# The three 3x3 convolutions of an attention block as matmuls over 42 channels x 3 tap rows

## The chip, the cores and the metric

One NeuronCore of a Trainium2 chip. Its engines are TensorE (PE; its weight loads are listed as PEld), VectorE (DVE), ScalarE (ACT), GpSimd (POOL) and SyncE (SP), which here only issues DMAs. Everything is float32. The metric is the device time of one execution in microseconds, the median over runs; lower is better.

## The reference, cut to what matters

The input is `x`, 8 images of 384 channels of 32 x 32 pixels. Four residual layers follow one another, each on a group norm of its input: attention with depthwise convolutions (layer 0), a mixture of experts, a ternary convolution block, and a deformable attention. Only the front of layer 0 is touched here:

```python
def _bn(x, g, b):                       # batch norm: statistics over images and pixels
    m = x.mean(axis=(0, 2, 3), keepdims=True); v = x.var(axis=(0, 2, 3), keepdims=True)
    return (x - m) * lax.rsqrt(v + EPS) * g[None, :, None, None] + b[None, :, None, None]

def _dwproj(x, dw, g, b, pw):           # depthwise 3x3, batch norm, gelu, 1x1 projection
    y = lax.conv_general_dilated(x, dw, (1, 1), ((1, 1), (1, 1)), feature_group_count=C, ...)
    y = jax.nn.gelu(_bn(y, g, b), approximate=False)
    return jnp.einsum('oc,bchw->bohw', pw, y)

q, k, v = (_dwproj(x, dw, g, b, pw) for each of three sets of weights)
# then softmax attention of 8 heads over the 1024 pixels, and an output projection
```

Each channel is convolved three times (for q, k and v) with nine weights of its own. No channel mixes with another. The batch norm needs the statistics of all eight images before the first gelu, so the convolutions are a stage of their own: every image is convolved, the raw result goes to DRAM, and only then does attention begin.

## The kernel before, in words

The kernel is written in a tile language that places instructions on the engines' queues; each engine takes its own queue in order, and waits are put in where a tile is read or its buffer is used again. `load_image` (line 145) brings an image in as three chunks of 128 channels x 1024 pixels, one DMA each. All DMAs are issued by SP.

The first stage works image by image:

- `gn_stats` (lines 77 to 121) makes the group norm's scale and shift: `bn_stats` and `bn_aggr` on DVE (lines 83 and 84), seven tiny matmuls `gna` (line 89), three small DVE steps (lines 97 to 101), seven tiny matmuls `gnb` (line 105), a power on POOL (line 75) and one more DVE step.
- `affine` (line 125, ACT) writes the normalized image into a zero-bordered tile `pad` of 34 x 34 pixels a channel. There are two `pad` tiles, used in turn.
- For each chunk of 128 channels, the k convolution runs on TensorE: nine products with diagonal 128 x 128 matrices `diag`, accumulated in a PSUM bank of 512 pixels, two banks a chunk (line 209), copied out by ACT (line 216). The matrices are built once on POOL (line 184).
- The q and v convolutions of the same chunk run on DVE, nine instructions each over 128 x 1024 pixels: line 223 for the first tap, line 225 for the other eight.
- `bn_stats` on DVE takes the statistics of each result (line 229), and a DMA stores it to `raw` in DRAM (line 232).

After the last image, `bn_params` (line 133 on) turns the statistics into scale and shift, which lie with the channels on partitions as the gelu wants them. Attention then loads its weights (lines 252 and 255), loads `g` from `raw` (line 145), applies gelu on ACT (line 265) and starts with the value projection `pv` on TensorE (line 275). From there on each of the eight images takes some 447 us in attention, and the other three layers follow.

Of the kernel before, what the change touches and what calls it, by code (L numbers as in the profile page):

```python
# [7 lines left out]
F32 = mybir.dt.float32  # L8
# [5 lines left out]
N = H * W            # tokens of one image  # L14
P = 128
KC = C // P          # channel chunks
HALF = N // 2        # one PSUM bank of fp32
NT8 = N // P         # token chunks of one image

# layer 0: attention of 8 heads of 48, each padded to 64 rows  # L20
NH0, HD0, NPAIR0 = 8, 48, 4
# layer 1: 4 experts
NE = 4
# layer 3: 6 heads of 64 over 16 x 16 sampled keys, 3 offset groups
NPAIR3, HS, LS, NG = 3, 16, 256, 3

# group norm: 32 groups of 12 channels; the chunk pairs that share a group
GN_C = C // 32
GN_PAIRS = {0: (0, 1), 1: (0, 1, 2), 2: (1, 2)}
RNE = 12582912.0     # 1.5 * 2^23: adding and subtracting rounds to the nearest even integer  # L30
# [3 lines left out]
def tile_kernel(ctx: ExitStack, tc: tile.TileContext, i: dict, out: bass.AP):  # L34
# [17 lines left out]
    def evac(dst, src):  # L52
        """A copy out of PSUM, by the Scalar and the Vector engine in turn."""
        flip[0] ^= 1
        if flip[0]:
            nc.scalar.copy(dst, src)  # L56
        else:
            nc.vector.tensor_copy(dst, src)  # L58
# [14 lines left out]
    def rsqrt(dst, var, n):  # L73
        """dst = var ** -0.5 for [P, n] tiles."""
        nc.gpsimd.tensor_tensor(dst, var, mhalf[:, :n], ALU.pow)

    def gn_stats(x, tag, pool=None):
        """Scale and shift [P, 2, KC] of the group norm of one image [P, KC, N]."""
# [6 lines left out]
        # group mean of the channels' means and variances  # L85
# [12 lines left out]
        # spread of the channels' means around the group's  # L98
# [30 lines left out]
    def bn_params(st, n, g, b, name):  # L129
        """Scale and shift [P, n] of a batch norm from the statistics [P, n, 2B, 6]."""  # L130
        mv = const.tile([P, n, 2], F32, name=f"bnmv_{name}")
        for j in range(n):
            nc.vector.bn_aggr(mv[:, j, :], st[:, j, :, :].rearrange("p a b -> p (a b)"))
        sc = const.tile([P, n], F32, name=f"bnsc_{name}")
        sh = const.tile([P, n], F32, name=f"bnsh_{name}")
        nc.vector.tensor_scalar(sh, mv[:, :, 1], 1e-5, None, ALU.add)
        rsqrt(sc, sh, n)
        nc.vector.tensor_tensor(sc, sc, g, ALU.mult)
        nc.vector.tensor_tensor(sh, mv[:, :, 0], sc, ALU.mult)
        nc.vector.tensor_tensor(sh, b, sh, ALU.subtract)  # L140
        return sc, sh
# [8 lines left out]
    def ternary(dst, w, shape, scale_ap):  # L150
        """dst = w + (clip(round(w * scale), -1, 1) - w)."""
# [10 lines left out]
    # ------------------------------------------------------------------  # L162
    # layer 0, part 1: group norm, three depthwise convolutions, their statistics
    # ------------------------------------------------------------------
    dw0 = load_const("dw0")        # [P, 3 convs, KC, 9]
    gb0 = load_const("gb0")        # [P, 2, 9]
    cst = const.tile([P, 9, 2 * B, 6], F32, name="cst")
    raw = [
        [dram.tile([P, KC, N], F32, name=f"raw{v}_{b}") for b in range(B)] for v in range(3)
    ]  # L170
    with ExitStack() as pa:
        wa = pa.enter_context(tc.tile_pool(name="a_w", bufs=1))
        xa = pa.enter_context(tc.tile_pool(name="a_x", bufs=2))
        ya = pa.enter_context(tc.tile_pool(name="a_y", bufs=3))
# [5 lines left out]
        # the key convolution runs on the tensor engine, as nine diagonal products  # L180
        diag = wa.tile([P, KC, 9, P], F32, name="diag")
        for c in range(KC):
            for t in range(9):
                nc.gpsimd.tensor_scalar(
                    diag[:, c, t, :], ident, dw0[:, 1, c, t : t + 1], 1.0, ALU.mult, ALU.mult
                )
        for b in range(B):
# [3 lines left out]
            pad = pads[b % 2]  # L191
            for c in range(KC):
# [6 lines left out]
            for c in range(KC):  # L199
                for v in (1, 0, 2):  # L200
                    y = ya.tile([P, H, W], F32, tag=f"y{v}", name=f"y{v}_{b}_{c}")
                    yf = y.rearrange("p h w -> p (h w)")
                    if v == 1:
                        for h in range(2):
                            pk = bank(f"pk{b}_{c}_{h}")
                            for t in range(9):
                                dy, dx = divmod(t, 3)
                                r0 = h * (H // 2) + dy
                                nc.tensor.matmul(  # L209
                                    pk,  # L210
                                    lhsT=diag[:, c, t, :],
                                    rhs=pad[:, c, r0 : r0 + H // 2, dx : dx + W],
                                    start=(t == 0),
                                    stop=(t == 8),
                                )
                            nc.scalar.copy(yf[:, h * HALF : (h + 1) * HALF], pk)
                    else:
                        for t in range(9):
                            dy, dx = divmod(t, 3)
                            src = pad[:, c, dy : dy + H, dx : dx + W]  # L220
                            w1 = dw0[:, v, c, t : t + 1]
                            if t == 0:
                                nc.vector.tensor_scalar(y, src, w1, None, ALU.mult)
                            else:
                                nc.vector.scalar_tensor_tensor(  # L225
                                    y, src, w1, y, ALU.mult, ALU.add
                                )
                    for h in range(2):
                        nc.vector.bn_stats(
                            cst[:, v * KC + c, 2 * b + h, :], yf[:, h * HALF : (h + 1) * HALF]  # L230
                        )
                    nc.sync.dma_start(out=raw[v][b][:, c, :], in_=yf)
    sc0, sh0 = bn_params(cst, 9, gb0[:, 0, :], gb0[:, 1, :], "qkv")

    # ------------------------------------------------------------------
    # layer 0, part 2: gelu, projections, attention, output projection
    # ------------------------------------------------------------------
    ost = const.tile([P, KC, 2 * B, 6], F32, name="ost")
    o_dram = [dram.tile([P, KC, N], F32, name=f"o_{b}") for b in range(B)]
    with ExitStack() as pb:  # L240
# [17 lines left out]
        for b in range(B):  # L258
            act = []
            for v in range(3):  # L260
                g = gp.tile([P, KC, N], F32, tag=f"g{v}", name=f"g{v}_{b}", bufs=2 if v < 2 else 1)
                load_image(g, raw[v][b])
# [7 lines left out]
            # values, tokens on partitions  # L270
# [91 lines left out]
    gbo = load_const("gbo")        # [P, 2, KC]  # L362
    sco, sho = bn_params(ost, KC, gbo[:, 0, :], gbo[:, 1, :], "out")

    # ------------------------------------------------------------------
    # weights of layers 1 to 3
    # ------------------------------------------------------------------
# [11 lines left out]
    # layer 2: ternary weights  # L379
# [4 lines left out]
    with tc.tile_pool(name="w2_raw", bufs=1) as wr:  # L384
        dw2 = load_w("dw2", wr)    # [P, KC, 9]
        pw2 = load_w("pw2", wr)    # [P, KC, C]
# [17 lines left out]
    # layer 3  # L404
# [5 lines left out]
    # bn3 columns: dw_b, bn_w, bn_b, bn_mean, bn_var  # L410
# [6 lines left out]
    # ------------------------------------------------------------------  # L417
    # layer 0's end and layer 1's routing
    # ------------------------------------------------------------------
    x1_dram = [dram.tile([P, KC, N], F32, name=f"x1_{b}") for b in range(B)]  # L420
    wk = wd.tile([P, B, 2, NT8], F32, name="wk")        # the two choices' weights by token
    pres = wd.tile([P, 2, NE], F32, name="pres")        # whether an expert is ever a choice
# [6 lines left out]
    with ExitStack() as pc:  # L429
# [3 lines left out]
        for b in range(B):  # L433
# [46 lines left out]
            for k in range(2):  # L480
# [4 lines left out]
                # of equal scores the lower index comes first  # L485
# [24 lines left out]
    # ------------------------------------------------------------------  # L510
    # layers 1 to 3, image by image
    # ------------------------------------------------------------------
# [6 lines left out]
    def layer1(b):  # L519
# [5 lines left out]
        # coefficients of the experts by token, then turned so that tokens lie along the free axis  # L525
# [84 lines left out]
    def layer3(b, xt):  # L610
# [15 lines left out]
        # the image with positions on partitions, to sample from  # L626
# [8 lines left out]
        # offsets: 5x5 depthwise convolution of stride 2  # L635
# [24 lines left out]
        # offsets and modulation of every sample, on all partitions  # L660
# [17 lines left out]
        # bilinear weights of a position for a sample: max(0, 1-|dy|) * max(0, 1-|dx|)  # L678
# [18 lines left out]
        # keys, scaled, and values with samples on partitions  # L697
# [85 lines left out]
def _chunks(w):  # L783
    """[K, M] -> [P, K / P, M]: rows by chunk of partitions."""
# [6 lines left out]
def _cols(v):  # L791
    """[C] -> [P, C / P]."""
# [3 lines left out]
def _layouts(a):  # L796
# [9 lines left out]
    # layer 0  # L806
    L["dw0"] = np.stack(
        [a[f"L0_conv_dw_{n}"].reshape(KC, P, 9).transpose(1, 0, 2) for n in "qkv"], axis=1
    )
    L["gb0"] = np.stack(  # L810
        [np.concatenate([_cols(a[f"L0_conv_{t}_{n}"]) for n in "qkv"], axis=1) for t in "gb"],
        axis=1,
    )
# [8 lines left out]
    # layer 1  # L822
# [8 lines left out]
    # layer 2  # L831
    L["dw2"] = a["L2_conv_w_dw"].reshape(KC, P, 9).transpose(1, 0, 2)
    L["pw2"] = _chunks(a["L2_conv_w_pw"].reshape(C, C).T)
    # layer 3
# [38 lines left out]
```

## Time and profile before

| | |
|---|---|
| median of 5 runs | 7619.18 us (7588.29 to 7625.57) |
| profiled execution, its own time | 7618.04 us |
| span of its trace, first to last instruction | 7616.3 us |
| mean granted TensorE clock | 0.862 |
| first convolution matmul starts | 22.41 us |
| last convolution matmul record begins | before 640.6 us |
| first matmul of attention (`pv`) | 685.82 us |

A trace is one execution. A group in it is named by line, engine and operation; "x864" counts the records of the group. A float32 matmul and its weight load each leave two records, so the 432 convolution matmuls of line 209 show as 864. "Idle before" is the time for which the engine did nothing ahead of the group, and what ended it. In the view of windows each engine's busy time in a stretch stands beside its instruction count, then the granted TensorE clock, the busy share of the 16 DMA engines and the GB/s that they moved. The records of matmuls overlap, so a matmul's own duration is longer than the step from one to the next.

### The profile page before, as it was taken

The numbers are of one execution on the slowest core, as the hardware profiler recorded it, in microseconds if no ns is written. First come the engines' busy times: TensorE is split into PE (matmuls) and PEld (weight loads), VectorE is DVE, ScalarE is ACT, GpSimd is POOL, SyncE is SP. The second block draws the span as 40 slices with busy tenths as digits, with TensorE's granted clock in tenths as the row PEclk, the third lists the DMA queues.
The fourth block names the chain that finished last, engine by engine and source line by source line (L and its number), as shares of the span: only waits on it lengthen the run. The fifth ranks groups of instructions, "written<-read, shape, count | busy, mean of one in ns | idle before, by whom it ended". The sixth has DMA issues, their size and how long they took to land.

```text
span 7616.3 us, 48331 instructions
## 1 busy us (share of the span) xinstructions
PE 6415.6 (84%) x18164; PEld 3010.5 (40%) x18164; DVE 3017.6 (40%) x4739; ACT 1957.4 (26%) x3391; POOL 913.6 (12%) x740
## 2 busy tenths in 40 slices
PE   6766999999999999999999569696969686878777
PEld 3333444444444444444444454343434343434333
DVE  8996333333333333333333321424242424242443
ACT  0002233323323332332222221222212121213123
POOL 0000111111111111111111000010101010101011
PEclk8887988898988889898898669898989898988888
DMA  2112000000000000000000420000000000000000
GB/s 92 77 69 97 0 25 9 17 17 0 33 0 25 9 17 17 1 34 0 6 3 4 164 100 0 9 9 9 9 9 9 9 9 9 9 9 9 0 9 9
DMA packets 52521, 178.74 MB, mean 23 GB/s; under 512 B 7352, under 2 KB 7612, under 8 KB 52032
## 3 DMA queue, kind: packets, MB, share of 16 engines
q1 hardware_dynamic: 52288, 175.65, 6.1%
q8 instruction: 144, 2.36, 0.1%
q14 instruction: 89, 0.73, 0.0%
HBM read 100.13 MB, written 75.50 MB: 23 GB/s over the span
## 4 chain that ended last, share of the span: by engine, by line
PE 73%; DVE 17%; ACT 5%; POOL 3%; issue 2%; DMA 1%; SPq 0%; ACTq 0%; DVEq 0%; POOLq 0%
PE pav L338 13%; PE s L316 12%; PE tp L332 8%; PE ph L556 7%; PE y L569 7%; PE pq L291 5%; DVE y L225 4%; DVE off L653 3%; DVE y L593 3%; PE po L351 2%; PE pv L275 2%; PE pav L754 2%; PE pk L209 2%; DVE mx L321 2%; PE pf L764 2%
## 5 line engine op out<-in xcount | busy, mean ns | idle before, releaser
L316 PE MATMUL s<-qk,qk 64*128 64x512 f32 x2048 | 1100.6, 681 | 97.8 <-ACT p L324 97.8
L338 PE MATMUL pav<-pt,vt 128*64 128x512 f32 x2048 | 962.4, 625 | 0.0
L327 POOL TENSOR_SCALAR p<-p,ri 128x1024 f32<-128x1024 f32 x512 | 571.3, 1119 | 2973.3 <-DVE ri L326 2968.7
L58 DVE COPY pt<-tp 128x512 f32<-128x512 f32 x608 | 419.2, 690 | 1052.1 <-PE tp L332 882.5
L321 DVE TENSOR_REDUCE mx<-s 128x1 f32<-128x1024 f32 x512 | 626.9, 1224 | 374.6 <-PE s L316 373.2
L332 PE MATMUL tp<-ident_sb,p 128*128 128x128 f32 x4096 | 676.2, 326 | 86.2 <-POOL p L327 86.2
L332 PEld LDWEIGHTS tp<-ident_sb,p 128*128 128x128 f32 x4096 | 564.9, 168 | 433.5 <-POOL p L327 274.4
L324 ACT ACTIVATE p<-s,mx 128x1024 f32<-128x1024 f32 x512 | 570.9, 1115 | 563.7 <-DVE mx L321 389.7
L56 ACT COPY pt<-tp 128x512 f32<-128x512 f32 x608 | 352.5, 585 | 893.5 <-PE tp L332 724.7
L316 PEld LDWEIGHTS s<-qk,qk 64*128 64x128 f32 x2048 | 353.3, 200 | 561.1 <-issue 302.8
L338 PEld LDWEIGHTS pav<-pt,vt 128*64 128x64 f32 x2048 | 284.0, 145 | 704.7 <-issue 659.0
L556 PE MATMUL ph<-h,w_sb 128*128 128x512 f32 x1152 | 558.8, 616 | 0.0
L569 PE MATMUL y<-hd,w_sb 128*128 128x512 f32 x1152 | 547.0, 612 | 0.0
L567 DVE TENSOR_TENSOR hd<-hd,cb 128x512 f32<-128x512 f32 x192 | 132.6, 691 | 850.6 <-ACT hd L564 850.6
L225 DVE SCALAR_TENSOR_TENSOR y<-pad,dw_sb,y 128x1024 f32<-128x1024 f32 x384 | 466.4, 1274 | 0.0
L209 PE MATMUL pk<-pad,diag 128*128 128x512 f32 x864 | 393.2, 619 | 23.0 <-ACT pad L125 23.0
L564 ACT ACTIVATE hd<-ph,b_sb 128x512 f32<-128x512 f32 x192 | 132.0, 687 | 925.8 <-PE ph L556 925.8
L556 PEld LDWEIGHTS ph<-h,w_sb 128*128 128x128 f32 x1152 | 221.0, 196 | 310.2 <-issue 267.5
L569 PEld LDWEIGHTS y<-hd,w_sb 128*128 128x128 f32 x1152 | 211.5, 193 | 299.9 <-issue 203.7
L602 PE MATMUL pw<-y,upw 128*128 128x512 f32 x288 | 164.7, 738 | 173.3 <-DVE y L593 173.3
L209 PEld LDWEIGHTS pk<-pad,diag 128*128 128x128 f32 x864 | 170.2, 198 | 240.1 <-issue 214.8
L741 POOL TENSOR_TENSOR p<-p,ri 128x1024 f32<-128x1024 f32 x96 | 181.0, 1893 | 497.8 <-DVE ri L740 494.1
(209 smaller groups left out, 6110.1 us busy)
## 6 DMA issues: line engine op xcount, KB each, us to landing
raw<-y SPq DMA_DIRECT2D x72, 512.0 KB, 2.6
g<-raw SPq DMA_DIRECT2D x72, 512.0 KB, 4.9
xa<-in_x_dram SPq DMA_DIRECT2D x24, 512.0 KB, 4.5
o<-ot SPq DMA_DIRECT2D x48, 256.0 KB, 2.0
xc<-in_x_dram SPq DMA_DIRECT2D x24, 512.0 KB, 4.4
oc<-o SPq DMA_DIRECT2D x24, 512.0 KB, 6.3
x<-xc SPq DMA_DIRECT2D x24, 512.0 KB, 2.9
x<-x SPq DMA_DIRECT2D x24, 512.0 KB, 4.7
```

What stands on the lines that cost most here:

```text
L58: nc.vector.tensor_copy(dst, src)
L209: nc.tensor.matmul(pk, lhsT=diag[:, c, t, :], rhs=pad[:, c, r0 : r0 + H // 2, dx : dx + W], start=(t == 0), stop=(t == 8),)
L225: nc.vector.scalar_tensor_tensor(y, src, w1, y, ALU.mult, ALU.add)
L291: nc.tensor.matmul(pq, lhsT=w_in[v][:, c, pr * P : (pr + 1) * P], rhs=act[v][:, c, h * HALF : (h + 1) * HALF], start=(c == 0), stop=(c == ...
L316: nc.tensor.matmul(s[:, ks], lhsT=qt[r, q0 : q0 + P], rhs=kt[r, ks], start=True, stop=True,)
L321: nc.vector.reduce_max(mx, s, AX.X, negate=True)
L324: nc.scalar.activation(p, s, AF.Exp, bias=mx, accum_out=rs)
L327: nc.gpsimd.tensor_scalar(p, p, ri, 1.0, ALU.mult, ALU.mult)
L332: nc.tensor.transpose(tp[:, k, :], p[:, kc * P : (kc + 1) * P], ident)
L338: nc.tensor.matmul(pav[r, :], lhsT=vt[:, kc, hd * 64 : (hd + 1) * 64], rhs=pt[:, kc, :], start=(kc == 0), stop=(kc == NT8 - 1),)
L556: nc.tensor.matmul(ph, lhsT=w1[:, e, c, dc * P : (dc + 1) * P], rhs=h1[:, c, hs], start=(c == 0), stop=(c == KC - 1),)
L569: nc.tensor.matmul(ys[m], lhsT=w2[:, e, dc, m * P : (m + 1) * P], rhs=hd, start=False, stop=(e == NE - 1 and dc == KC - 1),)
```

## The change: 42 channels, three tap rows and three convolutions to a matmul

The channels are cut into nine groups of 42 and a rest of 6 (`GC, NGC, GR = 42, 9, 6`). For a group, 126 partitions hold its 42 channels three times, the copies shifted by one image row each (`st`). One matmul with a 126 x 126 matrix takes the three rows of taps of one column offset for all three convolutions at once: its 126 outputs are q, k and v of the 42 channels. Three such matmuls, one for each column offset, finish a bank of 512 pixels. The six channels that are left over are stacked nine times (`sr`, 54 partitions) and take one matmul a bank.

DVE's tap instructions and POOL's diagonal matrices are gone; the matrices come from DRAM as an input of zeros and weights (`cw`, `cwr`). To get the stacks, the padded image is stored to DRAM (`hp`) and read back by three DMAs of 42 partitions x 9 groups x 1088 pixels and nine of 6 partitions. `stacks(b + 1)` is written ahead of image b's matmuls, and `st` has two buffers. ACT copies each bank out, DVE takes its statistics, and three DMAs store 42 rows each to `raw`. There are four `y` buffers.

The statistics now come out in stacked order, 126 partitions x 10 groups, so scale and shift are written to DRAM (`ssd`) and read back with channels on partitions, by 12 and 6 DMAs with elements of 4 bytes. The attention stage is as before, apart from the shape of `raw` in DRAM.

```diff
-        # the key convolution runs on the tensor engine, as nine diagonal products
-        diag = wa.tile([P, KC, 9, P], F32, name="diag")
-        for c in range(KC):
-            for t in range(9):
-                nc.gpsimd.tensor_scalar(diag[:, c, t, :], ident, dw0[:, 1, c, t : t + 1], ...)
-        for b in range(B):
+        def stacks(b):
             xt = xa.tile([P, KC, N], F32, tag="x", name=f"xa{b}")
             load_image(xt, x_img[b])
             ss = gn_stats(xt, f"a{b}")
             pad = pads[b % 2]
+            hp = dram.tile([C, NP_], F32, name=f"hp{b}")
             for c in range(KC):
                 affine(pad[:, c, 1 : H + 1, 1 : W + 1], xt[:, c, :]..., ss, c)
+                nc.sync.dma_start(out=hp[c * P : (c + 1) * P, :], in_=pad[:, c]...)
-            for c in range(KC):
-                for v in (1, 0, 2):
-                    y = ya.tile([P, H, W], F32, tag=f"y{v}", name=f"y{v}_{b}_{c}")
-                    if v == 1:
-                        for h in range(2):
-                            for t in range(9):
-                                nc.tensor.matmul(pk, lhsT=diag[:, c, t, :], rhs=pad[...], ...)
-                            nc.scalar.copy(yf[:, h * HALF : (h + 1) * HALF], pk)
-                    else:
-                        for t in range(9):
-                            if t == 0:
-                                nc.vector.tensor_scalar(y, src, w1, None, ALU.mult)
-                            else:
-                                nc.vector.scalar_tensor_tensor(y, src, w1, y, ALU.mult, ALU.add)
-                    for h in range(2):
-                        nc.vector.bn_stats(cst[:, v * KC + c, 2 * b + h, :], yf[...])
-                    nc.sync.dma_start(out=raw[v][b][:, c, :], in_=yf)
+            st = sa.tile([3 * GC, NGC, H, W + 2], F32, tag="st", name=f"st{b}")
+            for dy in range(3):
+                nc.sync.dma_start(
+                    out=st[dy * GC : (dy + 1) * GC].rearrange("p g h w -> p g (h w)"),
+                    in_=hp[: NGC * GC, dy * (W + 2) : (dy + H) * (W + 2)].rearrange(
+                        "(g c) n -> c g n", c=GC))
+            sr = sa.tile([9 * GR, H, W + 2], F32, tag="sr", name=f"sr{b}")
+            for t in range(9):
+                nc.sync.dma_start(out=sr[t * GR : (t + 1) * GR]..., in_=hp[NGC * GC :, o : o + nr])
+            return st, sr
+
+        nxt = stacks(0)
+        cw, cwr, gb0 = load_a("cw"), load_a("cwr"), load_a("gb0")
+        for b in range(B):
+            st, sr = nxt
+            if b + 1 < B:
+                nxt = stacks(b + 1)
+            for g in range(NGC + 1):
+                y = ya.tile([3 * nch, N], F32, tag="y", name=f"y{b}_{g}")
+                for h in range(2):
+                    if g < NGC:
+                        for dx in range(3):
+                            nc.tensor.matmul(pk[: 3 * nch, :], lhsT=cw[:, g, dx, :],
+                                rhs=st[:, g, rows, dx : dx + W], start=(dx == 0), stop=(dx == 2))
+                    else:
+                        nc.tensor.matmul(pk[: 3 * nch, :], lhsT=cwr, rhs=sr[:, rows, :W], ...)
+                    nc.scalar.copy(y[:, hs], pk[: 3 * nch, :])
+                    nc.vector.bn_stats(cst[: 3 * nch, g, 2 * b + h, :], y[:, hs])
+                for v in range(3):
+                    nc.sync.dma_start(out=raw[v][b][g * GC : g * GC + nch, :],
+                                      in_=y[v * nch : (v + 1) * nch, :])
+        scs, shs = bn_params(cst, NGC + 1, gb0[:, 0, :], gb0[:, 1, :], "qkv")
+        # 12 DMAs: scs, shs -> ssd in DRAM, channel by channel; 6 DMAs: ssd -> sc0, sh0 [P, 9]
```

## The prediction

> **What bounds the kernel now.** The page's 40 slices come first. Each is 190 us long.
>
> ```profile
> PE   6766999999999999999999569696969686878777
> DVE  8996333333333333333333321424242424242443
> ```
>
> DVE is nearly full in the first three and a half slices and nowhere else; PE has gaps there. The page's costliest groups say what DVE does:
>
> ```profile
> L225 DVE SCALAR_TENSOR_TENSOR y<-pad,dw_sb,y 128x1024 f32<-128x1024 f32 x384 | 466.4, 1274 | 0.0
> L209 PE MATMUL pk<-pad,diag 128*128 128x512 f32 x864 | 393.2, 619 | 23.0 <-ACT pad L125 23.0
> ```
>
> DVE's q and v taps never wait, and cost more than the whole k convolution on PE. The windows fix the edges: up to the first convolution matmul, to the last, and from there to the first `pv`.
>
> ```profile
> 0.00:22.40 22.40, 6.57 (x28) 6.27 (x28) 9.28 (x26) 2.58 (x3) 16.38 (x34) 1.00 0.48 172
> 22.40:640.60 618.20, 427.55 (x1060) 205.69 (x1060) 580.74 (x641) 54.38 (x70) 5.95 (x7) 0.81 0.18 73
> 640.60:685.80 45.20, 0.03 (x1) 0.00 (x0) 29.28 (x38) 9.93 (x10) 1.80 (x1) 0.53 0.56 222
> ```
>
> The columns are length, then PE, PEld, DVE, ACT, POOL, clock, DMA share, GB/s. Between 22.4 and 640.6 us DVE is busy 580.7 of 618.2 us (94%), PE 69%, the DMA engines 18%. The stage is bound by DVE, at some 82 us an image. After it PE idles 45 us: the last taps and statistics, scale and shift, then loads. The chain of waits shows this end:
>
> ```profile
> 667.00 9.23 DMA g<-raw
> ...
> 677.74 8.04 ACT g L265 x7
> ...
> 685.82 23.53 PE pv L275 x48
> ```
>
> Everything from `pv` on keeps its instruction order on every engine, so the forecast is when `pv` starts: 685.8 us now.
>
> **PE's new work.** Eight images of 9 groups x 2 banks x 3 matmuls and 2 for the rest: 8 x 56 = 448 matmuls, against 432. The `pv` row gives the step at full clock: 23.53 us hold a cold start, but later images show 20.60 us for 48 records, 0.429 us a record and 0.858 us a matmul. A matmul of 126 x 126 over 512 pixels has nearly the same shape; the row count hardly enters. So 448 x 0.858 = 384 us, 48.1 an image, if PE never waits. Of q, k and v together nothing is left to DVE but statistics: 160 x 0.68 (line 229) and 31 us of line 83, some 145 us in all. ACT gets 160 copies of 0.59 (line 216) and 28 us of `affine`: 122 us. Both lie beside PE. The 27 `diag` builds of POOL were done by 16 us and are worth nothing: `affine` at 21.1 us was later.
>
> **Cold starts.** After an idle stretch 54 records of line 209 take 26.1 to 26.5 us in the chain, against 54 x 0.429 = 23.2: 3.1 us lost whenever PE has stood.
>
> **The start.** The chain of the first image reaches the first `affine` at 21.1 us, with DVE work of image 1 in between that the new queue puts later; `xa` is also issued 0.9 us sooner (two constants less ahead of it). I take 18.4, and 3.5 us for the three `affine` (3.51 in the timeline): 21.9. Now new: the last `hp` store lands 2.6 us later (the `raw<-y` row), with issue at 25.5. Then three `st` transfers of 1.645 MB, 4.94 MB in all. No row shows a transfer of 42 rows. Bounds: 12 us at the 410 GB/s that queued loads reach at 670 to 690 us, 24.6 us at the 201 GB/s of a lone `raw` store (512 KB in 2.6 us). I take 18, halfway, since three are queued but each has a third of the rows, and 1.5 us to land: first matmul at 45 us, 3.1 us of cold start.
>
> [...]
>
> **Between images.** PE's queue puts the group norm of image b+2 between the matmuls of images b and b+1; in order, PE stands until it is through. The waits are these, in the present kernel:
>
> ```profile
> 150.84 0.95 PE L89 MATMUL gna_a<-mv_a,gmat_sb 128*128 128x2 f32 x8
> 174.98 1.44 PE L89 MATMUL gna_a<-mv_a,gmat_sb 128*128 128x2 f32 x6 [23.18 <-DVE mv_a L84]
> 178.20 3.12 PE L105 MATMUL gnb_a<-dm_a,gmat_sb 128*128 128x1 f32 x14 [1.78 <-DVE dm_a L101]
> 184.07 31.25 PE L209 MATMUL pk<-pad,diag 128*128 128x512 f32 x66 [2.75 <-ACT pad L125]
> ```
>
> Now they are covered by DVE's lead; then each counts. After images 0, 2 and 4 SP issues the `xa` loads only behind the last group's stores: copy 0.65, six issues of 0.43, landing 4.5 (the `xa` row), one chunk's statistics 1.5, then from the last `bn_aggr` to the end of `gnb` 6.1 (12.55 to 18.61 in the timeline): 15.3, with the cold start 18.4. Bounds by the landing's 3.4 to 8.8: 17.3 to 22.7. After 1, 3 and 5 the statistics are there already: gna 1.6, three DVE steps 0.7, gnb 3.1 and 2 of a possible 3.1 us cold: 7.5 (5.4 to 8.5). After 6 none. Sum 3 x 18.4 + 3 x 7.5 = 78 us.
>
> **Transfers under the matmuls.** A new image's stacks are issued some 7 us into the image before, and have 41 us left: 20 needed. Behind them in SP's queue stand the third store of group 0 and the rest; eight DMAs may be open, so SP stands until `st` has landed. `y` has four buffers: ACT's copy of group 4 (23 us in) waits for that store, and PE four banks later, at 31 us. With 18 us of transfer the store lands at 7 + 18 + 1.5 + 1.5 + 3 = 31: just free. With 24 it costs 6 us on each of seven images, 42 us. I book nothing. In all the stage moves 106 MB; over 16 engines at 24.8 GB/s each (63.6 MB at 22% share in the first 713 us) that is 267 us, under 511.
>
> **The end.** After the last matmul: copy, statistics, power, small DVE steps 4.9 us (the rows of lines 216, 229, 133 and 75). Then 12 stores and 6 loads with 4-byte elements, up to 378 in one. Lower bound: issue 12 x 0.43 and one landing of 1.9 us (`gbias`, 128 rows of 16 bytes): 7 us, and 2.6 for the loads' issue. Upper: 1.9 us for eight rows an engine is 0.24 us a row; six stores of 27 rows an engine give 38 us, the loads 34. I take 0.1 us a row, nearer to the low end since most of the 1.9 us is landing: 18 for the stores, 2 to issue the loads, 5 for what they hold up. Attention's own loads stand behind all of this on SP; from the first of them to `pv` were 21.4 us (664.4 to 685.8). Together 51 us (37 to 101), where 45 were.
>
> **Sum.** 45 + 3 + 384 + 78 + 51 = 561 us, against 685.8: 125 us less. The profiled execution took 7618.0, 1.1 us under the median: 7493, on the median's scale 7494 us.
>
> **Rivals.** *PE bound without the stalls* (chance 0.07): if the norm's matmuls found their inputs ready, 78 shrinks to 6 x 5 = 30 and the end to 37: 499, 7432 us. The queue order speaks against it.
>
> *DMA costs take much of it back* (0.20): stacks at 24.6 us, 42 us of stalls behind the stores, 4-byte elements at 0.24 us: 51 + 3 + 384 + 42 + 93 + 101 = 674, 7606 us; with half of these surcharges 7550. Nothing in the trace excludes them, but all at once is unlikely.
>
> *The 42-row transfers use few DMA engines* (0.06), and the kernel is slower. Every transfer now leaves 16 completion packets (123 DMAs of the first 713 us fit the 1968 packets under 512 B that no data explains), all on 128 rows. An image moves 9.6 MB in 42-row transfers and 3.3 MB in others: 9.6/(k x 24.8) + 8.4 us on k engines. Equal to now is a period of 73 us, k = 6. With k = 4 it is 105 us: 105 more at the start, 8 x 105 and 51, some 940 to 1000 us, that is 7870 to 7930. Its sign is DMA engines busy in part at a low total rate.
>
> [...]
>
> *The forecast case* has 0.67. Around it: low 45 - 3.5 at the start, 68 for the stalls, 37 at the end, 534: 7466. High, with stacks at 24.6 and half the other surcharges, 7550. For eight in ten I go from 7440, inside the first rival, to 7580. Below 0.3% (23 us) nothing can be told from no change. Faster 0.88; same 0.05, from the second rival's end; slower 0.07.
>
> **What would show it.** Right: PE's new line at 0.429 us a record, 896 of them; DVE under 30% in the stage; first `pk` near 45 us; PE waits of 15 us after images 0, 2, 4 named `mv_a` and of a few after 1, 3, 5; `pv` near 561. Wrong: `pk` waiting for `st` or ACT's `y` in every image (transfers bind), over 40 us between the last `bnsh` step and the first gelu load, or `pv` past 660.

## The result and the profile after

The changed kernel takes 7637.64 us (median of 32 runs, 7622.03 to 7650.69), the kernel before 7622.00 us (56 runs). The ratio is 1.0025, with a 95% interval of 1.002 to 1.003: 15.6 us slower. That is within the 0.3% (23 us) that the prediction called no change; it had put 0.88 on faster and 0.05 on this. The profiled execution has a span of 7640.7 us, and `pv` starts at 714.58 us where the prediction had 561 and the kernel before 685.82. From `pv` to the end it took 6926.1 us, against 6930.5 before, so the answer lies in the first stage.

The first slices of the page (190 us each), and the line of the convolution's matmuls:

```profile
PE   5776999999999999999999669696868787878777
DVE  2222333333333333333333331424242425242443
...
DMA  7664000000000000000000330000000000000000
...
L251 PE MATMUL pk<-st,cw_sb 126*126 126x512 f32 x864 | 405.6, 633 | 153.9 <-ACT y L262 126.2
```

VectorE has dropped to 2 tenths, as it should. TensorE has not risen: 5, 7, 7. The DMA engines show 7, 6, 6, 4. The matmuls were idle 126.2 us ahead of line 251 because ScalarE's copy into `y` (line 262) came late. The windows, with the columns of the prediction (length, PE, PEld, DVE, ACT, POOL, clock, DMA share, GB/s), cut at the first `pk`, the end of the last, and `pv`:

```profile
0.00:62.37 62.37, 13.23 (x56) 12.57 (x57) 12.43 (x34) 8.30 (x7) 7.82 (x8) 1.00 0.84 207
62.37:672.94 610.57, 452.86 (x1064) 207.51 (x1064) 140.40 (x248) 111.39 (x177) 5.10 (x6) 0.83 0.64 156
672.94:714.58 41.64, 0.01 (x2) 0.03 (x1) 2.60 (x8) 9.99 (x10) 1.95 (x1) 0.52 0.60 210
```

VectorE is busy 23% of the middle stretch, ScalarE 18%, TensorE 74%: no engine fills it. TensorE's timeline shows where it stands, here for two images of the eight:

```profile
62.37 33.59 PE L251 MATMUL pk<-st,cw_sb 126*126 126x512 f32 x72 [27.70 <-DMA sr<-hp]
114.91 17.49 PE L251 MATMUL pk<-st,cw_sb 126*126 126x512 f32 x36 [18.95 <-ACT y L262]
...
149.16 32.87 PE L251 MATMUL pk<-st,cw_sb 126*126 126x512 f32 x72
198.33 18.44 PE L251 MATMUL pk<-st,cw_sb 126*126 126x512 f32 x36 [16.29 <-ACT y L262]
```

Each image is cut in two: 72 records (six groups), a stop of 16.3 to 19.5 us, then 36. Seven images have such a stop, 126.2 us in all; the last, with no image behind it, has none. SyncE's issue timeline beside it (duration is the time from the first issue of a group to the end of its last) and its list of waits (total, times, longest) give the cause:

```profile
25.62 1.31 SPq L218 DMA_DIRECT2D st<-hp  x3
26.98 35.80 SPq L228 DMA_DIRECT2D sr<-hp  x9
...
70.86 0.76 SPq L265 DMA_DIRECT2D raw<-y  x2
71.79 1.96 SPq L218 DMA_DIRECT2D st<-hp  x3
73.79 37.56 SPq L228 DMA_DIRECT2D sr<-hp  x9
111.39 24.40 SPq L265 DMA_DIRECT2D raw<-y  x28
```

```profile
SPq L228 <- DMA st<-hp: 237.3, 24, 12.0
```

The nine small `sr` issues stand 35 to 38 us behind the three `st` transfers, one landing after the other: the waits for them last 9.9 us in the mean and 12.0 at most. In image 1 five of them go out by 77.6 us, eight open DMAs with the three `st`; the other four follow at 89.46, 98.50 and, two, 110.75 us. The third store of image 0's group 0 is among the 28 that are issued at 111.39 us, and TensorE moves again at 114.91. Both of ScalarE's and TensorE's waits follow:

```profile
ACT y L262 <- DMA raw<-y: 236.8, 33, 28.5
...
PE pk L251 <- ACT y L262: 126.2, 7, 19.5
```

So a stack takes some 36 us (4.94 MB, about 138 GB/s), not 18. Three windows, one inside each of the three transfers of the first image (TensorE has no `pk` to do yet), show their rates in the last column and the busy share of the DMA engines in the column before it:

```profile
28.00:38.00 10.00, 4.59 (x20) 4.42 (x20) 2.50 (x10) 1.96 (x2) 0.86 (x1) 1.00 0.91 131
40.00:50.00 10.00, 0.00 (x0) 0.00 (x0) 0.00 (x0) 0.00 (x0) 0.00 (x0) 1.00 0.91 191
52.00:60.00 8.00, 0.00 (x0) 0.00 (x0) 0.00 (x0) 0.00 (x0) 0.00 (x0) 1.00 0.85 128
```

The engines count as busy, and move a third to a half of the 410 GB/s that the trace of before had at 670 to 690 us. They are slow, not few: of packets under 512 B, of which the prediction counts one for each engine that a transfer uses, 14 stand at the end of the first transfer (37 to 41.5 us) and 14 at the end of the second (46.5 to 50 us).

### The profile page after: what moved, and what is told of

Same layout as the page of the kernel before. It is cut to its first block, busy times and chain, and to the rows that moved or that the text cites. A ratio compares the mean times of both kernels' runs of the same rounds, so it can differ in the third digit from the quotient of the medians.

```text
span 7640.7 us, 48573 instructions
## 1 busy us (share of the span) xinstructions
PE 6442.1 (84%) x18196; PEld 3018.4 (40%) x18196; DVE 2553.1 (33%) x4325; ACT 2019.8 (26%) x3503; POOL 904.3 (12%) x713
## 4 chain that ended last, share of the span: by engine, by line
PE 73%; DVE 11%; DMA 5%; ACT 5%; POOL 3%; issue 2%; SPq 0%; ACTq 0%; DVEq 0%; POOLq 0%
PE pav L391 12%; PE s L369 12%; PE tp L385 8%; PE ph L609 7%; PE y L622 7%; PE pq L344 5%; DMA st<-hp 3%; DVE off L706 3%; PE pk L251 3%; DVE y L646 3%; PE po L404 2%; PE pv L328 2%; PE pav L807 2%; DVE mx L374 2%; PE pf L817 2%
## 5 line engine op out<-in xcount | busy, mean ns | idle before, releaser
L251 PE MATMUL pk<-st,cw_sb 126*126 126x512 f32 x864 | 405.6, 633 | 153.9 <-ACT y L262 126.2
L251 PEld LDWEIGHTS pk<-st,cw_sb 126*126 126x126 f32 x864 | 173.2, 203 | 381.1 <-issue 247.5
L263 DVE BATCH_NORM_STATS2 cst<-y 126x6 f32<-126x512 f32 (+1 forms) x160 | 109.0, 690 | 448.2 <-ACT y L262 448.2
```

Source lines behind the costliest of these rows:

```text
L251: nc.tensor.matmul(pk[: 3 * nch, :], lhsT=cw[:, g, dx, :], rhs=st[:, g, rows, dx : dx + W], start=(dx == 0), stop=(dx == 2),)
```

## The experiments

The theory, A: the transfers are slow because each writes 42 neighbouring partitions; they hold SyncE's queue; the store of group 0 behind them keeps a `y` buffer, and TensorE waits. Rivals: the reading side in DRAM is at fault (B), only 14 engines take part (C), or four buffers would be short with any stack. Nothing after `pv` is meant to differ between the kernels that follow, yet that part took 6905 to 6937 us in their profiles, one execution each; so `pv` is the sharper measure of the stage, and the medians can differ by some 30 us for reasons that lie outside it.

### Spreading the rows over the partitions

```diff
-                    out=st[dy * GC : (dy + 1) * GC].rearrange("p g h w -> p g (h w)"),
+                    out=st[dy : 3 * GC : 3].rearrange("p g h w -> p g (h w)"),
-    L["cw"] = w.reshape(3 * GC, NGC, 3, 3 * GC)
+    L["cw"] = w.transpose(1, 0, 2, 3, 4, 5).reshape(3 * GC, NGC, 3, 3 * GC)
```

> The only edit: the three copies of a channel lie on partitions 3c, 3c+1, 3c+2 instead of c, 42+c, 84+c (rows of the matrices follow), so each st transfer writes every third partition from 0 to 125 instead of 42 neighbours. Bytes, DRAM addresses, transfer count and rows per transfer stay. Theory A (42 neighbouring partitions are what makes a transfer take 12 us): the three st transfers take 14 to 18 us instead of 36, the seven waits of 16 to 19 us in the middle of an image vanish (126 us in all), the first pk comes at about 45 us instead of 62, and the time falls by 130 to 145 us, to 7495 to 7510. Theory B (the DRAM side: rows that start at odd multiples of 136 bytes, read three times): unchanged, 7640. Theory C (only 42 rows in flight, 14 of 16 engines): unchanged, 7640.

Measured: 7520.83 us, ratio to before 0.9857 (0.984 to 0.9874); `pv` at 583.06 us. The same bytes, in the same order in DRAM, from the same queue; only the rows of the weights and the destination are permuted. Window of the first stacks, then SyncE's and TensorE's timelines:

```profile
28.00:35.00 7.00, 4.59 (x20) 4.42 (x20) 1.82 (x8) 0.00 (x0) 0.85 (x1) 1.00 0.88 356
```

```profile
28.14 14.72 SPq L228 DMA_DIRECT2D sr<-hp  x9
```

```profile
42.41 32.64 PE L251 MATMUL pk<-st,cw_sb 126*126 126x512 f32 x72 [8.65 <-issue]
79.63 17.37 PE L251 MATMUL pk<-st,cw_sb 126*126 126x512 f32 x36 [4.58 <-ACT y L262]
```

356 GB/s in place of 131 at the same share of busy engines, 14.7 us of standing in place of 35.8, the first matmul 20 us sooner, and the mid-image stops shrink from 126.2 to 25.1 us. They do not vanish, as A had it, and the median lies 11 us above A's range. What is slow is the placement of the rows, and A stands so far. B falls, since nothing on the DRAM side has changed, and so does C: the end of the first spread transfer (31.5 to 33.5 us) has 14 packets under 512 B, as before.

### The reading side: rows of DRAM at aligned starts

```diff
-NP_ = (H + 2) * (W + 2)
+NP_ = 1216
-                    out=hp[c * P : (c + 1) * P, :], in_=pad[:, c].rearrange("p h w -> p (h w)")
+                    out=hp[c * P : (c + 1) * P, : (H + 2) * (W + 2)], in_=pad[:, c]...
-                    in_=hp[: NGC * GC, dy * (W + 2) : (dy + H) * (W + 2)].rearrange(...
+                    in_=hp[: NGC * GC, 0 : H * (W + 2)].rearrange(...
```

A row of `hp` grows to 4864 bytes, and all three transfers read from its start. This kernel leaves out the shift by one image row between the three copies, so part of the convolution is missing; the transfers, their bytes and their partitions are the same.

> Rows of hp in DRAM are padded from 4624 to 4864 bytes and all three st transfers read from the row's start, so every row read begins at a multiple of 256 bytes (all three rows of taps then see the same image row, so part of the convolution is changed). Partitions stay. Theory A (neighbouring partitions): st stays at 34 to 36 us an image, time 7630 to 7645. Theory B (DRAM addresses): st falls to 14 to 20 us and the time to about 7500. Theory C: unchanged.

Measured: 7636.18 us, ratio 1.0021 (1.0011 to 1.0032). SyncE's waits for `st` barely move from 237.3 us, so where a row starts in DRAM is not what is slow:

```profile
SPq L228 <- DMA st<-hp: 234.3, 24, 11.6
```

### Eight y buffers for four, with the slow stacks

```diff
-        ya = pa.enter_context(tc.tile_pool(name="a_y", bufs=4))
+        ya = pa.enter_context(tc.tile_pool(name="a_y", bufs=8))
```

> Eight y buffers instead of four, nothing else. The stall in mid-image is ACT's copy of group 4 waiting for the third store of group 0, which SP issues only behind the st transfers. Theory A and B alike: st stays at 36 us, but now group 8 is the first that needs a used buffer, 41 us into the image, and SP is free again at about 45: the mid-image waits shrink from 16 to 19 us to under 5; the stores that pile up behind st are flushed in 10 us after it, and after images 0, 2, 4 the x loads behind them come later by up to 8 us each. Time 7530 to 7560. If the waits stay, the buffers are not what ACT waits for.

Measured: 7539.15 us, ratio 0.989 (0.987 to 0.991), `pv` at 622.57. `st` is as slow as it was, and TensorE runs through every image:

```profile
63.29 48.79 PE L251 MATMUL pk<-st,cw_sb 126*126 126x512 f32 x108 [28.13 <-DMA sr<-hp]
...
271.78 0.56 PE L92 MATMUL gna_a<-mv_a,gmat_sb 128*128 128x2 f32 x2 [25.33 <-DVE mv_a L87]
```

The second line is what it gave back. The stores are not gone, only late; the next `xa` loads stand behind them, and so the group norm between images 2 and 3 waits 25.3 us where it waited 8.3. The three long boundaries grow by 11 to 19 us each, where the expectation had up to 8.

### The stores on another queue

```diff
-                    nc.sync.dma_start(
+                    nc.scalar.dma_start(
                         out=raw[v][b][g * GC : g * GC + nch, :], ...
```

> The raw stores are issued by ACT instead of SP, so they no longer stand behind the st and sr issues in one queue; y has four buffers and st its slow layout. If the waits come from the order of SP's queue (the store sits behind three transfers of 12 us), they go although st stays slow: gain 100 to 126 us, 7515 to 7540, with st at 36 to 42 us since the stores now share the engines with it. If the DMA engines themselves are what the store has to wait for, the waits stay at over 10 us an image and the time at 7600 or more.

Measured: 7516.52 us, ratio 0.986 (0.9841 to 0.988), `pv` at 588.64. The stacks are still on neighbouring partitions and there are four `y` buffers, but no store stands behind a stack: TensorE runs through each image (at most 49.7 us for 108 records), with 12.6 us of short waits for `st` in all. So neither the slow transfer alone nor the four buffers alone cost the 126 us; it takes the queue that joins them. (The median is of two runs, 22 us apart.)

### Spread stacks and eight buffers

The two edits above together.

> Edit: the stacks on every third partition, and eight y buffers where there were four. Theory A (what is left of the waits in mid-image with the stacks spread, 25.1 us over seven images, is copies into y that stand behind stores behind the stacks): more buffers take these waits away, 7521 - 25 = 7496; some of it is given back, as with eight buffers alone, because the loads of the next image but one then stand behind stores that run later in the queue. 7490 to 7515, raw matmuls pk of an image in one stretch of 108. Rival B (the buffers are worth what they were worth beside the slow stacks, 98 us): 7425. Rival C (nothing is left for the buffers): 7521.

Measured: 7470.99 us, ratio 0.9803 (0.9786 to 0.9819), the lowest median of all; `pv` at 550.60, 32 us ahead of the spread version. 25 of these are the stops that are gone; by `pv` A's size holds. The median lies 19 us below A's range: it gained 17 us more than `pv`, and the profiles put these after `pv`, in unchanged code (6912 us against 6937). The stretch per image in the timeline:

```profile
109.03 49.35 PE L251 MATMUL pk<-st,cw_sb 126*126 126x512 f32 x108
158.31 1.89 PE L259 MATMUL pk<-sr,cwr_sb 54*18 54x512 f32 x4
165.57 48.39 PE L251 MATMUL pk<-st,cw_sb 126*126 126x512 f32 x108
213.89 1.89 PE L259 MATMUL pk<-sr,cwr_sb 54*18 54x512 f32 x4
232.49 49.06 PE L251 MATMUL pk<-st,cw_sb 126*126 126x512 f32 x108
```

Two boundaries can be read here: 5.4 us from 160.2 to 165.57, and 16.7 us from 215.8 to 232.49.

### The outputs spread as well

With the stacks spread and four buffers, the three convolutions' outputs are interleaved too (`in_=y[v : 3 * nch : 3, :]`, with the columns of `cw`, `cwr` and the rows of `gb0` permuted to match, and the `ssd` stores reading every third row).

> Edit: the stacks on every third partition, and the three convolutions' outputs too, so that each raw store reads 42 rows of y that lie three partitions apart; four y buffers. Theory A (the price of a copy with 42 neighbouring partitions holds for its reading side as well as for its writing side): a store's time falls, the stacks beside which stores still run (21.7 to 24.9 us before images 1, 2, 4 and 6) come nearer to the 15 us of the first image, and the mid-image waits of 25.1 us shrink: 7490 to 7515. Rival B (a store reads 172 KB of 42 rows at a rate that DRAM or the queue sets): 7521, the waits unchanged.

Measured: 7487.19 us, ratio 0.9822 (0.9807 to 0.9837), `pv` at 564.67, and the mid-image stops are 8.7 us in place of 25.1. With the stacks alone spread, those for image 1 took 22.55 us (first line, the spread version); with the outputs spread as well they take 14.75 (second line, this kernel):

```profile
53.49 22.55 SPq L228 DMA_DIRECT2D sr<-hp  x9
```

```profile
55.60 14.75 SPq L228 DMA_DIRECT2D sr<-hp  x9
```

So A's sign came, but its reason, that a copy pays for neighbouring rows when it reads them, is not borne out by the stores themselves. Behind these stacks SyncE lets a series of stores go. In the first 12 us of it they move 233 GB/s at a busy share of 0.75 with neighbouring rows (first line, the spread version), and 196 at 0.61 with rows three apart (second line, this kernel): no slower, and about the same for each busy engine.

```profile
76.00:88.00 12.00, 8.37 (x16) 3.73 (x17) 3.91 (x6) 3.32 (x6) 0.00 (x0) 0.86 0.75 233
```

```profile
70.40:82.40 12.00, 12.00 (x29) 5.26 (x28) 3.96 (x6) 3.32 (x6) 0.00 (x0) 1.00 0.61 196
```

Nor do the stores run beside the slow stack: by the packets of the spread version the two stores ahead of it were through at 53.4 us, and the stack went on to 75. What differs is its start. In the spread version the stacks of images 1, 2, 4 and 6 began 0.3 to 0.9 us before the last packet of these stores had ended, and took 21.7 to 24.9 us; those of images 3, 5 and 7, and all seven in this kernel, began 0.2 to 0.8 us after it, and took 14.5 to 17.7. Whether this overlap is the cause, and how so short a one would slow a whole stack, was not tested.

### Loads and group norm an image earlier

On top of spread stacks and eight buffers, `load_x(b + 2)` is issued ahead of image b's groups, and `gn_stats` of image b+2 is emitted before group 6.

> Edit: the stacks on every third partition, eight y buffers, each image's load issued one image earlier, ahead of the stores of the image before, and its group norm emitted before the seventh group of that image. Theory A (between two images TensorE waits for the load, the group norm's matmul and its short chain, since they stand behind the stores and the statistics of the image before): the three long boundaries of 16.6 us come down to the 5.4 us of the short ones, 34 us, and the mid-image waits of 25 us are gone: 7521 - 59 = 7462, 7455 to 7485. Rival B (the group norm in mid-image holds up VectorE or the SP queue, and TensorE with them): 7490 to 7510.

Measured: 7477.00 us, ratio 0.9809 (0.9795 to 0.9824), `pv` at 555.49. The boundaries are gone (the next `pk` starts as the rest ends), and TensorE stops in mid-image instead, here in image 1:

```profile
111.29 31.17 PE L259 MATMUL pk<-st,cw_sb 126*126 126x512 f32 x72
153.24 17.91 PE L259 MATMUL pk<-st,cw_sb 126*126 126x512 f32 x36
```

Between 142.5 and 153.24 us stand VectorE's statistics of the new image and 28 records of small matmuls, in order on TensorE. 10.8 us on each of five images, and 6.9 on the first, come to 61 us, where the six boundaries had 65; little is won. The start lost 9 us to the earlier load (first `pk` at 51.5 us). The median lies in A's range, but the larger part of A's account, the boundaries' 34 us, was not gained: `pv` is 5 us later than without the edit, and what B named, the group norm in mid-image, is why.

### The same, with the stacks on neighbouring partitions

> Edit: as the version with early loads and eight y buffers, but the stacks on neighbouring partitions as the change has them. Theory A (the slow stacks cost time only through what stands behind them, and at the start, where nothing covers them): 20 us above the spread version, the first image's difference, so 7475 to 7505, and the matmuls of each image in one stretch. Rival B (the slow stacks also cost by the path of the next image, from its first store to hp to its first matmul): more than 40 us above the spread version, 7505 to 7540.

Measured: 7572.57 us, ratio 0.9935 (0.9912 to 0.9957), `pv` at 665.14, 110 us behind the spread version. 14 us of it are the start. The rest: the last of the three `xa` loads is issued behind the slow `st`, and the group norm in mid-image waits for it, 22 to 27 us a stop in place of 7 to 11. The time lies past even B's range, and the path is not the one B named (from the store to `hp` to the first matmul). A slow transfer at the head of one queue is paid by whatever stands next, a store or a load.

### The group norm in five pieces

`stacks(0)` before `load_x(1)`, and the group norm of image b+2 emitted one piece ahead of each of the groups 5 to 9.

> Edit: as the version with early loads on spread stacks, but the first image's stacks are emitted before the second image's load, and the group norm of the image after next is emitted in five pieces, one before each of the groups 5 to 9, so that TensorE's two sets of its 14 small matmuls find their operands ready. Theory A (in the version with early loads TensorE stands 10.8 us in the middle of each of six images, because the group norm's matmuls, emitted in one piece, wait in order for VectorE's statistics; about 4.6 us of these are the matmuls themselves): 6 x 6 = 36 us less there, and the first matmul pk at 42 instead of 51.5 us: pv at about 510, 7477 - 45 = 7432, 7420 to 7450. Rival B (the gaps are the small matmuls' own time or a wait for the load, which the pieces do not shorten): only the 9 us of the start, 7465 to 7475.

Measured: 7484.87 us, ratio 0.9826 (0.9801 to 0.9851), `pv` at 554.68. That is 53 us above A's figure and 10 above B's range. Of the start 6 us came back (45.3 us), but an image still takes 62 to 64 us:

```profile
212.60 0.35 PE L93 MATMUL gna_a<-mv_a,gmat_sb 128*128 128x2 f32 x2 [2.92 <-DVE mv_a L87]
212.81 1.10 PE L267 MATMUL pk<-st,cw_sb 126*126 126x512 f32 x2
213.90 1.16 PE L93 MATMUL gna_a<-mv_a,gmat_sb 128*128 128x2 f32 x6
214.92 7.58 PE L267 MATMUL pk<-st,cw_sb 126*126 126x512 f32 x10
```

The pieces did not run where they were emitted: VectorE makes the statistics of all three chunks in one series, from 210.94 to 215.24 us, when eight of the image's groups are through. So the run does not test five spread pieces. TensorE's wait for the statistics stays (2.9 us), and after it ten records of `pk` take 6 to 7.6 us, where 0.429 us a record would be 4.3. That is a cold start: from 215 to 221 us the granted clock is 0.50, from 221.1 to 222.4 it is 1.00. How to put this group norm under the matmuls for nothing was not found.

## Why the prediction was wrong

Its sum, term by term, against the profile of after:

| term | predicted | measured |
|---|---|---|
| first `pk` | 45 | 62.4 |
| 448 matmuls and one cold start | 384 + 3 | 384 + 2.6 |
| between images | 78 (3 x 18.4 and 3 x 7.5) | 64.2 of gaps and 6 cold starts, 80 |
| stores behind the stacks | 0 | 126.2 of stops and 7 cold starts, 144 |
| last `pk` to `pv` | 51 | 41.6 |
| `pv` | 561 | 714.6 |

The gaps are read from the timeline: 14.9, 16.6 and 16.6 us after images 0, 2 and 4, and 5.4 after 1, 3 and 5. The cold start is what is left of 714.6 without these gaps, the stops, the two ends and 384, over 14 starts (one, six and seven): 2.6 us, between the 2 and the 3.1 that were used. The granted clock shows it: 0.56 from 114.91 to 119 us, just after the first stop, and 1.00 in the next 6 us. The 384 are 896 records at 0.429 us.

**The step that failed** is the size of the stacks' transfer, "I take 18, halfway". It took 36. The upper bound of 24.6 us came from a lone store of 128 rows, and a transfer that writes 42 neighbouring partitions (128 to 191 GB/s) is slower than both of the rows that the bounds were made of (201 and 410). From this one input come both big misses: 17 us at the start, and the 144 us under "I book nothing".

**The mechanism was in the text** and its formula was right: a stack's time + 7 + 1.5 + 1.5 + 3, less 31. With 36 us it gives 18 us a stop; measured were 16.3 to 19.5. That it comes so near is in part luck, since two of its terms were off and nearly cancel: the stacks were issued 8.6 to 12.1 us into an image, not 7, and TensorE stood after 32.6 to 33.6 us, not 31, which leaves the cold start out. It was priced at 24 us, 42 in all, and put in a rival of 0.20, of which the forecast's range took half. The queue with four buffers had no slack at the value taken (31 us against 31): a booking of nothing that hung on an unmeasured rate.

**The rival with few DMA engines** did not happen: the share of 0.85 to 0.91 in the transfers' windows, and the 14 small packets at the end of a transfer, leave no room for four or six of sixteen engines. Its six engines would have moved 149 GB/s, near the 138 measured, but it is the engines' rate that is low, not their number.

**Right** were the step of 0.429 us (46.62 us for the last image's 108 records, 896 records in all), VectorE's 23%, the named waits on `mv_a` after images 0, 2, 4, and the two sizes of boundary. The end was 9 us shorter than taken: from the first `ssd` store (677.37 us) to the issue of attention's first load (691.83) took 14.5 us, where the prediction had 25. Its 0.1 us a row was too dear. The 27 rows an engine of its upper end are 378 elements over 14 engines, which no row of the trace of before shows. After has 2424 packets of 4 bytes at 677 to 686 us for 2304 elements stored; the other 120 fit 14 for each of the six large stores and 6 for each of the small ones.

**What the runs leave open.** That placement sets the rate is shown by the spread version: 344 to 356 GB/s for its first stacks, where the change's neighbouring rows had 131, 191 and 128, with 14 small packets at the end of a transfer in both. By what mechanism neighbouring partitions slow a transfer was not shown; nor why the second of the three is faster than the other two, nor why the stores, which read the same blocks of partitions, were not slow (233 GB/s).

**Where the gain is.** The change's matmuls are worth what was forecast: with the stacks spread and eight buffers `pv` is at 550.6 us, 10 before the forecast, and the kernel at 7470.99. What stays of TensorE's idle time there is the 42.4 us ahead of the first `pk`, the group norm between the images, and the 40.6 us before `pv`.

## What to carry to other kernels

When a layout puts a block of neighbouring partitions in each transfer, price it by a transfer of that very layout, or spread the rows (every third partition instead of a third of the partitions): here that is an edit of one slice and of the weights' order, and some 131 us of the stage (`pv` from 714.6 to 583.1). A queue that issues in order hands a slow transfer on to whatever stands behind it (here a stop of 16.3 to 19.5 us in each of seven images), so for each long transfer name the next store and the next load behind it, and ask by how much their slack exceeds the error of the transfer's time. Where a zero in the sum rests on a rate that no row shows, put the range's edge at the price of that zero being wrong by a factor of two.

## What was not expected of the hardware

The first image's transfers of 42 neighbouring partitions moved 128 to 191 GB/s, those of 42 rows three partitions apart 344 to 356, with the DMA engines' busy share between 0.85 and 0.91 in both: that share does not tell a fast transfer from a slow one. Stores that read 42 neighbouring partitions were not slow (233 GB/s at a share of 0.75). Twelve stores and six loads with 4-byte elements, up to 384 in one, took 14.5 us together from the first issue to the next queue entry.
